# Three moves in the order of work of a state-space layer: softplus pieces, direct products, and spread ahead of decay

## The chip, the cores and the metric

The kernel runs on one core of a Trainium2 chip. The metric is the device time of one execution in microseconds (us), lower is better. The engines are TensorE (PE in the profile; PEld is its loading of weights), VectorE (DVE), ScalarE (ACT), GpSimd (POOL) and SyncE (SP), which issues the DMAs. Each works through its own queue in order and waits for others by semaphores.

## The reference

The input is x of shape (16, 128, 56, 56), all in float32. Two layers follow one another. The first is a block with a depthwise position convolution, layer norm, attention over windows of 8 by 8 pixels (each window attends to the four windows that fit it best), and an MLP. The change doesn't touch it. The second layer is:

```python
y = conv3x3(x) + conv_b                          # 128 -> 128 channels
seq = y.reshape(B * H * W, 8, 16)                # 50,176 sequences: 8 tokens of 16
out = mamba(seq)
out = group_norm(out, 4 groups) ; return x + silu(out)

def mamba(seq):
    xi, z = split(seq @ in_proj_w.T)             # 32 and 32
    xc = silu(causal_conv4(xi) + conv1d_b)
    dt, Bm, Cm = split(xc @ x_proj_w.T)          # 1, 16 and 16
    dt = softplus(dt * dt_proj_w + dt_proj_b)    # 32 per token
    dA  = exp(dt[..., None] * -exp(A_log))       # 32 x 16 per token
    dBx = dt[..., None] * Bm[:, :, None, :] * xc[..., None]
    h = 0
    for l in range(8):                           # the scan over the tokens
        h = dA[l] * h + dBx[l]                   # 32 x 16 states
        ys[l] = sum(h * Cm[l], over the 16)
    return ((ys + D * xc) * silu(z)) @ out_proj_w.T
```

## The kernel before

The first layer takes the first 3.2 ms of the span and the second layer the rest. The second layer (`layer1`, from line 711) works in 112 **row groups**: 16 images with 7 groups each (`g` 0 to 6), 448 sequences a group. A group's states at one token are 32 x 16 = 512 rows of 448, so four tiles of 128 partitions. They are worked on in two halves (`jp` 0 and 1) of two tiles each.

The main loop (lines 1192 to 1213) runs over groups `i` and, in each, over 14 **steps** `k`. Step `k` advances token `l = 1 + k // 2` in half `jp = k % 2`. Its work, in the order in which it is written and so queued:

- **advance** (lines 938 to 947, VectorE): the product `a * h` of the decay with the state of the token before (L946) and the add of the new input (L947). At token 7 (steps 12 and 13) a single product (L944) does it.
- **inject** for step `k + 4` (L936, VectorE): the spread product in PSUM times the gate Bm, written into a tile `h` as that token's new input.
- **decay** for step `k + 2` (L918, TensorE): dt times A into a PSUM tile `a`. There are two such tiles, so it waits until the advance of step `k` has read the older one.
- **spread** for step `k + 5` (L929, TensorE): dt * xc copied to the 128 rows of a tile. There is one PSUM tile `x`, so it waits for the inject of this step.
- **the exponential of the decay** (L921, ScalarE), in place in `a`.
- **weigh** at odd steps (L951, GpSimd): a token's state times the gate Cm, into `cst`.
- then what `work(i, k)` (lines 1077 to 1175) lists for the step, first VectorE's, then TensorE's, with the ScalarE work that reads their PSUM, then GpSimd's.

A decay and a spread of one step are four instructions each, two per tile of the half; each uses 32 rows of the array, and the two work on different halves.

`work` carries the current group `p`, the next one `nxt`, the one after that `far`, and older ones. For `nxt`:

- **rate** (lines 843 to 852, steps 1 and 2) is the dt product with wv into PSUM bank `pq0`, and ScalarE's absolute value `e` and positive part `dt`.
- **rate_exp** (854 to 857) and **rate_log** (859 to 862) are the rest of the softplus on ScalarE, two instructions each, for the two halves `h` of the tokens. **rate_sum** (864 to 870) is its four sums and products on GpSimd, at steps 6 and 8.
- **gate** (872 to 882, step 3) is the Bm and Cm products, ScalarE's two copies (L880) and their way through DRAM.
- **inner** (833 to 838) is a product into `pq0` and `pq1` and its SiLU on ScalarE: for `zs` of `nxt` at step 4 and for `xc` of `far` at step 12. A SiLU needs another activation table than exponentials and logarithms, so each call loads a table (L837), runs two SiLUs, and loads the first table back (L145).
- **product** (894, GpSimd, step 10) and **direct** (898 to 900, TensorE, step 13) prepare, for tokens 0 and 7, Bm * Cm summed over the 16 states, in bank `pq0`. **direct_mul** (902 to 908, two L905 on VectorE) multiplies it with dt * xc into `ud`.

For `p` and the group before it, **gather** (955 to 963, TensorE) sums `cst` over the states into `pq1`, **skip** (965) adds D * xc there, **collect** (970, VectorE) adds `ud`, **gated** (975, GpSimd) multiplies with silu(z) and **project_out** (980 to 1009) is the output product. One tap or two of the next image's 3x3 convolution (L787) stand on TensorE at steps 5 to 10. At an image's end group statistics and the normalisation come in: `group_mean` (L1027) and `group_var` (L1038) on TensorE, two large SiLUs (L1061) on ScalarE at step 12, and sums on GpSimd (L1068).

What sets the order is the order in which the program is written. `_chain` (lines 148 to 158) ties each engine's instructions to that order, SyncE's too; no planner moves them. The tiles `h` come from a pool of four. In the order of their first writing they are those of tokens 2, 3, 4, 5, 6, the next group's 0, then 7, then the next group's 1, and so on, so that the inject of step 12, which starts the next group's token 1, takes the tile of token 5.

Of the kernel before, what the change touches and what calls it, by code (L numbers as in the profile page):

```python
# [711 lines left out]
def layer1(ctx: ExitStack, tc: tile.TileContext, x1, t, out):  # L712
# [45 lines left out]
    for w, name in ((wx, "b_kx"), (wv, "b_dtw")):  # L758
        k = w1.tile(list(w.shape), F32, tag="fold", name=name)
# [124 lines left out]
    def bring(p, k, tokens):  # L884
        n = len(tokens)
        tile_ = w3.tile([P, 2, BLK], F32, tag="bc"[k] + "b", name=f"{'bc'[k]}b_{p['n']}_{tokens[0]}")
        src = p["dram", k][:, tokens[0] : tokens[0] + n, :].rearrange("s l n -> s (l n)")
        nc.sync.dma_start(
            tile_[:, 0:n, :].rearrange("p l n -> p (l n)"), src.unsqueeze(1).to_broadcast([16, 8, n * BLK])
        )  # L890
        for i, l in enumerate(tokens):
            p["gate", k, l] = tile_[:, i, :]
# [20 lines left out]
    def decay(p, l, jp):  # L913
        h, l4 = divmod(l, 4)
        a = p["a", l, jp] = ps_a.tile([P, 2, 512], F32, tag="a", name=f"a_{p['n']}_{l}_{jp}")[:, :, 0:BLK]
        for k in range(2):
            rows = slice(32 * (2 * jp + k), 32 * (2 * jp + k) + 32)
            nc.tensor.matmul(a[:, k, :], lhsT=adec[rows, l4, :], rhs=p["dt"][rows, h, :], start=True, stop=True)  # L918

    def decay_exp(p, l, jp):  # L920
        nc.scalar.activation(p["a", l, jp], p["a", l, jp], AF.Exp)  # L921
# [16 lines left out]
    def advance(p, l, jp):  # L938

        a, before = p["a", l, jp], p["h", l - 1][:, own(jp), :]  # L940
        if l == 7:
            if jp == 0:
                p["h", l] = w4.tile([P, 4, BLK], F32, tag="h", name=f"h_{p['n']}_{l}")
            nc.vector.tensor_mul(p["h", l][:, own(jp), :], a, before)  # L944
        else:
            nc.vector.tensor_mul(a, a, before)  # L946
            nc.vector.tensor_add(p["h", l][:, own(jp), :], a, p["h", l][:, own(jp), :])  # L947
# [129 lines left out]
    def work(i, k):  # L1077


        def at(n):  # L1080
            return groups[n] if 0 <= n < len(groups) else None

        p, nxt, far, prev = at(i), at(i + 1), at(i + 2), at(i - 1)
        pe, dve, pool = [], [], []
# [35 lines left out]
            pool.append(partial(store, three["b"], 1, k // 2 - 1))  # L1120

        if p:
            if k == 1:
                dve.append(partial(direct_mul, p))
            if k == 7:
                pe.append(partial(skip, p, 0))
            if k in (8, 9, 10):
                pe.append(partial(gather, p, k - 7))
            if k == 12:
                dve.append(partial(collect, p, 0))  # L1130
            if k == 13:
                pe += [partial(skip, p, 1), partial(gather, p, 4)]
                pool.append(partial(gated, p, 0))
            if k in (2, 6):
                bring(p, 0, {2: (4, 5), 6: (6,)}[k])
            if k in (1, 5, 9):
                bring(p, 1, {1: (3, 4), 5: (5, 6), 9: (7,)}[k])

        if nxt:
            if k in (1, 2):  # L1140
                pe.append(partial(rate, nxt, k - 1))
            if k in (2, 3):
                pe.append(partial(rate_exp, nxt, k - 2))
            if k in (3, 4):
                pe.append(partial(rate_log, nxt, k - 3))
            if k in (6, 8):
                pool.append(partial(rate_sum, nxt, k // 2 - 3))
            if k == 3:
                pe += [partial(gate, nxt, 0), partial(gate, nxt, 1)]
            if k == 4:  # L1150
                pe.insert(0, partial(inner, nxt, "zs", wz, w2, 0.0))
            if k == 7:
                bring(nxt, 0, (0, 1))
            if k == 8:
                bring(nxt, 1, (1, 2))
            if k == 11:
                bring(nxt, 0, (2, 3))
            if k == 10:
                pool.append(partial(product, nxt))
            if k == 13:  # L1160
                pe.append(partial(direct, nxt))

        if p and k in (5, 6, 7, 8, 9, 10) and p["b"] + 1 < NB:
# [28 lines left out]
    for i in range(-2, len(groups) + 3):  # L1192
        for k in range(14):
            now = 0 <= i < len(groups)
            if now:
                advance(*state_step(i, k))
            inputs = input_step(i, k + 4) if now or (i == -1 and k >= 10) else None
            if inputs:
                inject(*inputs)
            decays = state_step(i, k + 2) if now or (i == -1 and k >= 12) else None  # L1200
            if decays:
                decay(*decays)
            inputs = input_step(i, k + 5) if now or (i == -1 and k >= 9) else None
            if inputs:
                spread(*inputs)
            if decays:
                decay_exp(*decays)
            if now and k % 2:
                weigh(groups[i], 1 + k // 2)
            pe, dve, pool = work(i, k)  # L1210
            for part in (dve, pe, pool):
                for step in part:
                    step()
# [37 lines left out]
```

## Time and profile before

| | us |
|---|---|
| median of three runs | 8841.8 |
| lowest and highest | 8837.53 and 8855.01 |
| the profiled execution's own time | 8843.74 |
| its span, first to last instruction | 8841.9 |
| mean granted TensorE clock (1 is full) | 0.966 |
| first product of the first group's advance, from the span's start | 3250.8 |

The costliest groups of the second layer, as the profile lists them:

| line, engine | what | count | mean, ns |
|---|---|---|---|
| L951 POOL | weigh | 784 | 3996 |
| L936 DVE | inject | 1568 | 1083 |
| L946 DVE | advance, product | 1344 | 1091 |
| L947 DVE | advance, add | 1344 | 1092 |
| L921 ACT | exponential of the decay | 1568 | 900 |
| L918 PE | decay | 6272 | 606 |
| L929 PE | spread | 6272 | 608 |
| L787 PE | convolution tap | 2016 | 580 |

In a row of the timeline the first number is the start in us from the span's start and the second is the duration; in brackets stand the engine's idle time before the row and what ended it. A row with x2 or x4 has several like instructions merged, one behind the other. Where an engine is idle but another sets the pace, the idle time costs nothing.

### The profile page before, as it was taken

How to read it: one execution, taken by the hardware profiler on the slowest of the kernel's cores; microseconds unless marked ns; L12 is line 12 of the kernel's file. 1: busy time of each engine (PE TensorE's matmuls, PEld its weight loads, DVE VectorE, ACT ScalarE, POOL GpSimd, SP SyncE). 2: the span in 40 equal slices, each digit the busy share in tenths (PEclk: the TensorE clock that was granted, in tenths of full speed). 3: DMA queues.
4: the chain of work that ended last, by engine and by line, in shares of the span. 5: the costliest groups of instructions: out<-in, count | busy, mean ns of one | idle time of the engine just before them, and what ended most of it. 6: DMA issues, size and time to landing. Idle time of an engine off the chain costs nothing.

```text
span 8841.9 us, 151450 instructions
## 1 busy us (share of the span) xinstructions
PE 8013.1 (91%) x52860; PEld 3322.9 (38%) x52860; DVE 7764.8 (88%) x10358; ACT 5603.8 (63%) x10516; POOL 7035.4 (80%) x5664
## 2 busy tenths in 40 slices
PE   6999999999999879999999999999999999999987
PEld 3444444444444433333333333333333333333332
DVE  7999999999999839898898988988988989889887
ACT  4776777777777636666655665665656665666654
POOL 5878888878888328888888888888888888888887
PEclk8999999999999989999999999999999999999997
DMA  2333333333333222333333333333333333333332
GB/s 62 85 85 89 87 87 87 86 87 89 87 86 88 76 61 80 93 90 83 90 90 83 91 83 99 84 88 93 87 85 86 88 92 91 82 98 85 87 89 69
DMA packets 764424, 757.86 MB, mean 86 GB/s; under 512 B 188688, under 2 KB 663952, under 8 KB 761616
## 3 DMA queue, kind: packets, MB, share of 16 engines
q1 hardware_dynamic: 763664, 748.18, 32.8%
q8 instruction: 422, 6.91, 0.3%
q14 instruction: 338, 2.77, 0.1%
HBM read 439.61 MB, written 102.76 MB: 61 GB/s over the span
## 4 chain that ended last, share of the span: by engine, by line
PE 31%; ACT 24%; DVE 21%; POOL 11%; issue 10%; DMA 1%; SPq 0%; ACTq 0%; POOLq 0%; DVEq 0%
PE pq L787 8%; PE a L918 8%; ACT a L921 5%; DVE a L946 5%; DVE lepe L460 4%; DVE h L947 4%; POOL xh L263 4%; PE pq L960 4%; POOL e L379 4%; PE x L929 3%; ACT L837 3%; DVE h L936 3%; POOL tap L261 2%; ACT L145 2%; DVE sst L363 2%
## 5 line engine op out<-in xcount | busy, mean ns | idle before, releaser
L951 POOL TENSOR_TENSOR cst<-h,cb 128x1792 f32<-128x1792 f32 x784 | 3129.4, 3996 | 855.1 <-DVE h L947 580.4
L921 ACT ACTIVATE a<-a 128x896 f32<-128x896 f32 x1568 | 1404.3, 900 | 1772.7 <-PE x L929 1174.8
L936 DVE TENSOR_TENSOR h<-x,bb 128x896 f32<-128x896 f32 x1568 | 1697.6, 1083 | 276.9 <-PE x L929 145.6
L918 PE MATMUL a<-dt,adec 32*128 32x448 f32 x6272 | 1659.7, 606 | 214.4 <-DVE h L947 213.5
L946 DVE TENSOR_TENSOR a<-a,h 128x896 f32<-128x896 f32 x1344 | 1466.3, 1091 | 358.1 <-ACT a L921 357.5
L460 DVE SCALAR_TENSOR_TENSOR lepe<-vpad,lep,lepe 128x448 f32<-128x448 f32 x2688 | 1718.4, 678 | 0.6
L929 PE MATMUL x<-dtx,amask 32*128 32x448 f32 x6272 | 1664.8, 608 | 25.5 <-DVE h L936 24.5
L947 DVE TENSOR_TENSOR h<-a,h 128x896 f32<-128x896 f32 x1344 | 1467.0, 1092 | 45.8
L379 POOL TENSOR_SCALAR e<-e,sst,zero 128x256 f32<-128x256 f32 x1568 | 861.6, 560 | 451.4 <-DVE sst L375 396.6
L369 ACT ACTIVATE e<-ps,sst 128x256 f32<-128x256 f32 x1568 | 728.8, 469 | 544.5 <-DVE sst L363 493.6
L787 PE MATMUL pq<-x1pad,conv 128*128 128x448 f32 x2016 | 942.8, 580 | 59.5 <-ACT gst L1039 32.5
L918 PEld LDWEIGHTS a<-dt,adec 32*128 32x128 f32 x6272 | 484.2, 188 | 1247.4 <-DVE h L947 578.4
L263 POOL TENSOR_TENSOR xh<-xh,tap 128x448 f32<-128x448 f32 x735 | 841.4, 1145 | 42.5
L960 PE MATMUL pq<-cst,sel 128*32 128x448 f32 x6272 | 750.9, 564 | 1.5 <-POOL cst L951 1.5
L401 PE MATMUL ptt<-ident,e 128*128 128x128 f32 x3136 | 546.4, 285 | 92.3 <-POOL e L379 75.2
L363 DVE TENSOR_REDUCE sst<-ps 128x2 f32<-128x512 f32 x784 | 540.4, 689 | 86.3 <-PE ps L357 63.8
L929 PEld LDWEIGHTS x<-dtx,amask 32*128 32x128 f32 x6272 | 485.0, 189 | 339.8 <-DVE h L936 333.7
L357 PE MATMUL ps<-sel,q 32*64 32x256 f32 x6272 | 540.8, 413 | 68.2 <-ACT e L369 61.7
L261 POOL TENSOR_SCALAR tap<-xpad,pos,zero 128x448 f32<-128x448 f32 x735 | 533.6, 726 | 34.4
L787 PEld LDWEIGHTS pq<-x1pad,conv 128*128 128x128 f32 x2016 | 349.2, 194 | 497.4 <-issue 441.9
L401 PEld LDWEIGHTS ptt<-ident,e 128*128 128x128 f32 x3136 | 367.9, 142 | 416.5 <-POOL e L379 238.0
L407 ACT COPY att<-ptt 128x512 f32<-128x512 f32 x784 | 458.6, 585 | 48.0 <-PE ptt L401 40.3
(164 smaller groups left out, 12292.7 us busy)
## 6 DMA issues: line engine op xcount, KB each, us to landing
sel<-kv SPq DMA_DIRECT2D x3136, 64.0 KB
bb<-db SPq DMA_DIRECT2D x336, 448.0 KB
cb<-dc SPq DMA_DIRECT2D x336, 448.0 KB
xpad<-x SPq DMA_DIRECT2D x32, 784.0 KB
x<-r SPq DMA_DIRECT2D x112, 224.0 KB
x1pad<-x SPq DMA_DIRECT2D x16, 1568.0 KB
db<-bs SPq DMA_DIRECT2D x112, 224.0 KB
dc<-cs SPq DMA_DIRECT2D x112, 224.0 KB
```

The source lines that it names most:

```text
L263: nc.gpsimd.tensor_add(im["xh"][i], im["xh"][i], held["tap"])
L379: nc.gpsimd.tensor_scalar(e, e, im["st", w][:, 2, p : p + 1], zero, ALU.mult, ALU.add)
L460: nc.vector.scalar_tensor_tensor(out, src, lep[:, k : k + 1], acc, ALU.mult, ALU.add)
L787: nc.tensor.matmul(pc, lhsT=conv[:, k, :], rhs=pad[:, 8 * i + dy : 8 * i + dy + 8, dx : dx + W], start=(k == 0), stop=(k == 8),)
L918: nc.tensor.matmul(a[:, k, :], lhsT=adec[rows, l4, :], rhs=p["dt"][rows, h, :], start=True, stop=True)
L921: nc.scalar.activation(p["a", l, jp], p["a", l, jp], AF.Exp)
L929: nc.tensor.matmul(x[:, k, :], lhsT=mask[rows, l4, :], rhs=p["dtx"][rows, h, :], start=True, stop=True)
L936: nc.vector.tensor_mul(p["h", l][:, own(jp), :], px["x"], weight)
L946: nc.vector.tensor_mul(a, a, before)
L947: nc.vector.tensor_add(p["h", l][:, own(jp), :], a, p["h", l][:, own(jp), :])
L951: nc.gpsimd.tensor_mul(c, p["h", l], p["gate", 1, l].unsqueeze(1).to_broadcast([P, 4, BLK]))
L960: nc.tensor.matmul(py[32 * j : 32 * j + 32], lhsT=sel[:, l4, :], rhs=p["c", l][:, j, :], start=False, stop=(l % 4 == 3), skip_group_check= ...
```

## The change

There are three moves; no instruction is added or taken away.

- In the softplus of the next group, the first half's `rate_exp` stays at step 2 and its `rate_log` goes from step 3 to step 5. The second half's `rate_exp` goes from step 3 to step 6 and its `rate_log` from step 4 to step 7. `rate_sum` stays at steps 6 and 8.
- `direct_mul` goes from step 1 to step 0. `direct`, which makes its input, stays at step 13 of the group before, but ahead of that step's `skip` and `gather`. Only ahead of the very first group does it stand where it was.
- In each step of the main loop, `spread` is queued ahead of `decay`.

```diff
@@ work
         if p:
-            if k == 1:
+            if k == 0:
                 dve.append(partial(direct_mul, p))
...
             if k == 13:
+                if nxt:
+                    pe.append(partial(direct, nxt))
                 pe += [partial(skip, p, 1), partial(gather, p, 4)]
                 pool.append(partial(gated, p, 0))
...
         if nxt:
             if k in (1, 2):
                 pe.append(partial(rate, nxt, k - 1))
-            if k in (2, 3):
-                pe.append(partial(rate_exp, nxt, k - 2))
-            if k in (3, 4):
-                pe.append(partial(rate_log, nxt, k - 3))
+            if k in (2, 6):
+                pe.append(partial(rate_exp, nxt, k // 4))
+            if k in (5, 7):
+                pe.append(partial(rate_log, nxt, k // 2 - 2))
...
-            if k == 13:
+            if k == 13 and not p:
                 pe.append(partial(direct, nxt))
@@ the main loop
             decays = state_step(i, k + 2) if now or (i == -1 and k >= 12) else None
-            if decays:
-                decay(*decays)
             inputs = input_step(i, k + 5) if now or (i == -1 and k >= 9) else None
             if inputs:
                 spread(*inputs)
             if decays:
+                decay(*decays)
                 decay_exp(*decays)
```

## The prediction

> **What bounds it now.** I read the page first, then the busy times of one image's seven row groups, then the waits and the rows of one ordinary group. The page says that no engine is the limit throughout:
>
> ```profile
> PE 8013.1 (91%) x52860; PEld 3322.9 (38%) x52860; DVE 7764.8 (88%) x10358; ACT 5603.8 (63%) x10516; POOL 7035.4 (80%) x5664
> ...
> PE 31%; ACT 24%; DVE 21%; POOL 11%; issue 10%; DMA 1%; SPq 0%; ACTq 0%; POOLq 0%; DVEq 0%
> ```
>
> The chain hands over between four engines, so single waits count. The next view has busy time by stretch, one stretch per row group of the second layer (first product to first product):
>
> ```profile
> core 0: us, PE busy (x) PEld busy (x) DVE busy (x) ACT busy (x) POOL busy (x), PEclk, DMA share, GB/s
> ...
> 5728.02:5781.39 53.37, 47.99 (x237) 17.12 (x236) 44.23 (x46) 30.19 (x45) 41.63 (x25) 0.87 0.25 70
> 5781.39:5841.52 60.13, 50.97 (x233) 17.50 (x232) 45.18 (x48) 35.26 (x46) 47.49 (x23) 0.86 0.42 105
> ...
> 5888.93:5936.54 47.61, 45.24 (x236) 16.15 (x235) 44.71 (x48) 29.46 (x42) 40.32 (x19) 1.00 0.28 78
> ```
>
> Five of an image's seven groups are like the last (47.4 to 47.6 us, TensorE clock 1.00); two, after an image's end, are longer and run at 0.87 and 0.86. In the ordinary group VectorE works 44.7 of 47.6 us. Its waits there:
>
> ```profile
> DVE a L946 <- ACT a L921: 2.3, 2, 1.5
> DVE h L936 <- PE x L929: 0.2, 1, 0.2
> ```
>
> So two products wait for a decay exponential, 0.76 and 1.53 us. From here times of this group are us after its first product, at 5888.93. The rows of VectorE (timeline) give the places, steps 1 and 7, and where the direct products stand, behind step 1:
>
> ```profile
> 5892.90 1.10 DVE L946 TENSOR_TENSOR a<-a,h 128x896 f32<-128x896 f32 x1 [0.76 <-ACT a L921]
> ...
> 5896.04 1.27 DVE L905 SCALAR_TENSOR_TENSOR ud<-pq,vec,dtx 128x448 f32<-128x448 f32 x2
> ...
> 5915.02 1.10 DVE L946 TENSOR_TENSOR a<-a,h 128x896 f32<-128x896 f32 x1 [1.53 <-ACT a L921]
> ```
>
> ScalarE's rows say why step 7 is late: its exponential (first of the x2) stands behind a table load, two SiLUs, a load back, and two softplus pieces.
>
> ```profile
> 5908.53 0.92 ACT L921 ACTIVATE a<-a 128x896 f32<-128x896 f32 x1
> 5909.46 1.28 ACT L837 ACT_TABLE_LOAD   x1
> 5910.76 0.98 ACT L837 ACTIVATE zs<-pq 128x448 f32<-128x448 f32 x2
> 5911.76 1.28 ACT L145 ACT_TABLE_LOAD   x1
> 5913.05 0.67 ACT L861 ACTIVATE u<-u,neg 128x448 f32<-128x448 f32 x1
> 5913.63 0.56 ACT L862 ACTIVATE ln<-e 128x448 f32<-128x448 f32 x1
> 5914.09 1.70 ACT L921 ACTIVATE a<-a 128x896 f32<-128x896 f32 x2
> ```
>
> **The change, part by part.** It adds and removes no instruction; ACT, PE and DVE rows move. POOL's and SP's order stays, and each DMA keeps its place.
>
> *Spread ahead of decay.* Before, a decay product may start when its step's add is done, a spread product 1.0 us later, when the inject is done. Now the decay stands behind the spread and both start on the inject. They use different row strips and run side by side (rows at 5889.19 and 5889.20: both over in 1.03), so a spread ends as before and a decay ends about 1.0 later wherever TensorE used to wait; where TensorE was behind they already ran together and nothing changes. What waits behind is the step's exponential. In the ordinary group the exponentials of products 3, 4 and 5 end 2.3, 2.6 and 1.6 us before their products, so 1.0 is covered; product 6 had 0.8, but its exponential was held by ScalarE's queue, which is emptied below. Behind TensorE work at step 12 the decay moves from 5886.21 to 5886.5, so that the first SiLU burst and the exponential behind it (product 1) come 0.35 later: a cost of 0.35 if nothing fills it.
>
> *Direct products one step sooner.* Two L905 take 1.19 start to start (5896.04 to the product at 5897.23). They now stand between step 0's inject (ends 3.21) and product 1. That product waits until 3.97 now and until about 4.32 with the 0.35; the two L905 end the same gap at 4.32. Their TensorE product moves ahead of the skip, which waits for the second SiLU (5890.71); the direct one needs the first alone and is over near 2.6, before 3.1. So product 2, now at 8.30, comes at 4.33 + 3.13 (the distance of two products that do not wait, 5904.02 to 5907.15) = 7.46: a gain of 0.84. Without that cover the L905 cost their 1.19 at step 0 as they did at step 1: a loss of 0.35, the other end.
>
> *Softplus pieces.* Four rows of 0.5 to 0.65 leave step 3, two leave step 4; pairs go to steps 5, 6 and 7, where the exponentials now wait for TensorE 1.7 to 3.5 us. The chain to product 7: inject 8 ends 17.47 (0.84 earlier), spread and decay 1.09, exponential 0.95, so the first load starts at 19.53 (now 20.53); load 1.29, SiLUs 0.98, load 1.29, and directly the exponential, 23.11 to 24.01. Product 7 starts at 24.05 instead of 26.09: 2.04 in all, of which 1.20 is the softplus move. If the load stayed where it is, only the 1.04 of the two rows behind the SiLUs would come, and none if they merely came back ahead of a later exponential; step 8's is next and is needed 1 us after it ends.
>
> *What is late next.* GpSimd: its first softplus sum needs the logarithm's companion (L861), which now runs behind exponential 7 and ends at 24.7; GpSimd was free at 24.6 in the old frame and would be at 23.75. From the first sum's start to the end of cst of token 5 it is never idle (5913.54 to 5930.94: 17.4). The inject of step 12 reuses the h buffer which that cst reads. Now it ends at 42.0 and the inject starts at 44.07; with the change 24.75 + 17.4 = 42.15 against about 41.9, when VectorE and TensorE would be ready. So the inject comes at 42.2: 1.87 gained in this group, 1.65 in the 47.38 kind (inject at 43.85). TensorE's stretch from step 7 to 12 (3.55 a step, 5918.32 on) starts 2.05 earlier and is not the last. I take 1.75 a group. Ends: 2.04 (GpSimd in time) and 0.5 (head lost, burst mostly).
>
> *The two long groups of each image.* In the first TensorE idles 2.32 and runs at half speed behind it; I take 1.5, between 0 and 3.0 (this group takes 53.4 in some images, 50.3 in others). In the second, product 1 waits 6.65 behind the normalisation; the L905 move into that wait (1.19), but TensorE then works cold and the later decays no longer use its idle time: 0.7, between -1.0 and 2.4.
>
> *Sum.* 80 x 1.75 + 16 x (1.5 + 0.7) = 140 + 35 = 175. The profiled execution took 8843.7 (span 8841.9), 1.9 over the median of the three runs, 8841.8. 8841.8 - 175 = 8667.
>
> **The clock.** The row against this change is TensorE's clock:
>
> ```profile
> 5742.97 0.38 PE L1027 MATMUL pq<-mv,gmask 128*128 128x1 f32 x2 [1.31 <-ACT dt L852]
> ...
> 5744.54 3.08 PE L876 MATMUL pq<-xc,wbc 128*64 128x448 f32 x8
> ```
>
> After an idle time of 1.31 us the gate product takes 3.08 instead of 1.72 (5904.57). In the new order TensorE idles 1.0 to 1.1 at steps 2 and 3 of every group (dt product over at 12.8, next inject at 13.8), where it idled at most 0.5. For: the size. Against: it does the same products in a step of the same 3.13, only closer together, while around the 1.31 one spread came 3.6 after the other. The Trainium skill, TensorE: Matmul & The Clock Gate, section "Why this matters for your kernels", asks only that there be no idle gaps over about 3 us, as the clock falls after one idle window; by that rule an idle 1.1 costs nothing and the sum stays 8667, by the row above it may cost half a window or more. The trace does not agree with the page here, since 1.31 was enough.
>
> **Rivals.** (A) GpSimd takes the place more fully: its spans are rough, and each 0.1 us on that run of 17.4 costs 80 x 0.1 = 8 us. At 1 us more the gain is 0.75 a group: 8842 - 60 - 12 = 8770. For: it is packed from 24.6 to 51. Against: before step 6 it idles 1.6, 3.5 and 1.7 us a group. (B) Slower, by the clock: if it halves at steps 3 to 5 of every ordinary group, a stretch like the one above (slow from about 5743.9 to 5747.3, where the next pair is at full speed again: 3.4) costs TensorE 1.7, two cost 3.4. One just eats the 1.75; from two on it decides: 80 x 1.65 - 35 = +97, 8939. (C) Slower, by the later decays: direct products not ready (+0.35) and the burst no sooner because load and exponential wait for the decay: 112 x 0.35 = +39, 8881. It decides where a product's lead is under 1.0; only 6, of those not already waiting, is. (D) Nothing: the two waits are refilled by one another, 8842.
>
> **Numbers.** Chances: forecast 0.69, A 0.15, B 0.08, C 0.05, D 0.03. Faster 0.84, within 0.2% (18 us, about what a measurement tells from no change) 0.03, slower 0.13. The low end takes 2.04 a group and the upper bounds of the long ones: 163 + 86 = 249, 8593, rounded to 8590; the high end goes past A to 8790, leaving B, C and D out. The forecast's own range is 8600 to 8740.
>
> **What would show it.** Right: no wait at step 1 and about 0.4 at step 7; L905 straight behind step 0's inject; ordinary groups of 45.7 to 45.9; a short wait of step 12's inject for GpSimd; clock 1.00 there. Wrong: cold gate products (3.1) in ordinary groups, a wait at step 6, or exponential 7 waiting for L918.

## The result and the profile after

The changed kernel takes 8627.45 us (median of four runs, 8618.99 to 8630.68); the kernel before took 8841.59 beside it (8837.53 to 8855.01). The ratio is 0.9754, with a 95% interval from 0.9737 to 0.9771: faster by 214 us. The forecast was 8667, a gain of 175. The profiled execution has a span of 8617.2 us, 224.7 under the 8841.9 of before; all times taken from its rows are compared with that.

The page of the changed kernel, busy times and the shares of the chain that ended last:

```profile
PE 7449.8 (86%) x52860; PEld 3113.3 (36%) x52860; DVE 7758.7 (90%) x10358; ACT 5643.5 (65%) x10516; POOL 7025.9 (82%) x5664
...
DVE 32%; POOL 25%; PE 16%; ACT 13%; issue 12%; DMA 2%; SPq 0%; POOLq 0%; ACTq 0%; DVEq 0%
```

No engine has less work, but TensorE is busy for 563 us less (a spread and a decay that run side by side count once), and the chain has moved: TensorE's share fell from 31% to 16%, ScalarE's from 24% to 13%, and GpSimd's rose from 11% to 25%. The same by row group, for the three groups shown before the change (busy time of each engine, the granted TensorE clock, and the transfers):

```profile
core 0: us, PE busy (x) PEld busy (x) DVE busy (x) ACT busy (x) POOL busy (x), PEclk, DMA share, GB/s
5615.15:5664.04 48.89, 44.02 (x237) 15.48 (x236) 44.09 (x46) 30.32 (x45) 42.06 (x25) 0.93 0.28 76
5664.04:5720.19 56.15, 43.55 (x233) 15.07 (x232) 44.96 (x47) 35.34 (x46) 48.82 (x24) 0.91 0.45 112
...
5765.94:5811.69 45.75, 40.32 (x236) 14.22 (x235) 44.67 (x47) 29.80 (x42) 40.12 (x19) 1.00 0.30 81
```

The ordinary group (last row) went from 47.61 to 45.75, and VectorE works 44.7 of it. Its waits are down to two short ones:

```profile
DVE a L946 <- ACT a L921: 0.4, 1, 0.4
DVE h L936 <- POOL cst L951: 0.3, 1, 0.3
```

The wait at step 1 is gone and the one at step 7 fell from 1.53 to 0.38; a short one for GpSimd is new. VectorE's rows give the places (first number: start from the span's start; this group's first product starts at 5765.94):

```profile
5765.94 1.09 DVE L946 TENSOR_TENSOR a<-a,h 128x896 f32<-128x896 f32 x1
...
5769.07 1.26 DVE L905 SCALAR_TENSOR_TENSOR ud<-pq,vec,dtx 128x448 f32<-128x448 f32 x2
5770.31 1.10 DVE L946 TENSOR_TENSOR a<-a,h 128x896 f32<-128x896 f32 x1
...
5790.08 1.10 DVE L946 TENSOR_TENSOR a<-a,h 128x896 f32<-128x896 f32 x1 [0.38 <-ACT a L921]
...
5808.16 1.09 DVE L936 TENSOR_TENSOR h<-x,bb 128x896 f32<-128x896 f32 x1 [0.29 <-POOL cst L951]
```

The two direct products (L905) stand straight behind step 0's inject, product 1 follows them at 4.37 after the first, product 7 comes at 24.14, and the inject of step 12 at 42.22. ScalarE's rows of the burst in the same group:

```profile
5784.62 0.90 ACT L921 ACTIVATE a<-a 128x896 f32<-128x896 f32 x1 [1.52 <-PE a L918]
5785.56 1.28 ACT L837 ACT_TABLE_LOAD   x1
5786.86 0.98 ACT L837 ACTIVATE zs<-pq 128x448 f32<-128x448 f32 x2
5787.85 1.28 ACT L145 ACT_TABLE_LOAD   x1
5789.15 0.90 ACT L921 ACTIVATE a<-a 128x896 f32<-128x896 f32 x1
5789.96 0.66 ACT L861 ACTIVATE u<-u,neg 128x448 f32<-128x448 f32 x1
```

The exponential of step 7 now stands directly behind the load back, and the logarithm pieces behind it.

Where the 224.7 us lie, by the place of a row group in its image (mean from first product to first product; the long groups are the second and third places of an image, since the end of the image before is worked off there):

| groups | before, us | after, us | gain in all, us |
|---|---|---|---|
| 70 ordinary ones of the 14 inner images | 47.55 | 45.77 | 125 |
| second place of the 14 inner images | 51.58 | 48.19 | 48 |
| third place of the 14 inner images | 58.73 | 56.38 | 33 |
| first image, all seven | 48.31 | 45.78 | 18 |
| last image, first six | 48.98 | 48.88 | 1 |
| from the last group's first product to the end of the span | 86.51 | 85.23 | 1 |

The ordinary groups are what the forecast said. The long ones of these 14 images gained 80 us where it said 31 (35 for all 16), and that is the whole of the difference to the 224.7 us of the profile.

### The profile page after: what moved, and what is told of

It reads as the page before. It is cut to its first block, busy times and chain, and to the rows that moved or that the text cites. A ratio compares the mean times of both kernels' runs of the same rounds, so it can differ in the third digit from the quotient of the medians.

```text
span 8617.2 us, 151466 instructions
## 1 busy us (share of the span) xinstructions
PE 7449.8 (86%) x52860; PEld 3113.3 (36%) x52860; DVE 7758.7 (90%) x10358; ACT 5643.5 (65%) x10516; POOL 7025.9 (82%) x5664
## 4 chain that ended last, share of the span: by engine, by line
DVE 32%; POOL 25%; PE 16%; ACT 13%; issue 12%; DMA 2%; SPq 0%; POOLq 0%; ACTq 0%; DVEq 0%
DVE h L936 10%; DVE a L946 7%; POOL cst L951 5%; PE x L929 5%; POOL xh L263 5%; POOL e L379 4%; DVE h L947 4%; DVE lepe L460 3%; POOL tap L261 3%; ACT a L921 3%; POOL dtx L870 2%; PE pq L960 2%; PE pq L787 2%; ACT L145 2%; DVE sst L363 2%
## 5 line engine op out<-in xcount | busy, mean ns | idle before, releaser
L947 DVE TENSOR_TENSOR h<-a,h 128x896 f32<-128x896 f32 x1344 | 1467.2, 1092 | 46.1
```

## The experiments

The theory to test is the prediction's own: the gain is the sum of a shorter burst (softplus), a filled wait (direct products), and next to nothing for the spread, until GpSimd is late. The rivals are that one move carries all of it, and that TensorE's clock decides (rival B). Each run below says how it differs from the changed kernel or from the one before. Each time stands beside one of the kernel before, measured on the same chip: 8841.0 for the three runs with one move undone and the early logarithm, 8853.8 for the run with TensorE kept busier and the three with one move alone, 8842.0 for the next three, 8851.5 for the last. Between these sets the ratios are compared.

### One move undone

**Without the softplus move.** The changed kernel, with:

```diff
-            if k in (2, 6):
-                pe.append(partial(rate_exp, nxt, k // 4))
-            if k in (5, 7):
-                pe.append(partial(rate_log, nxt, k // 2 - 2))
+            if k in (2, 3):
+                pe.append(partial(rate_exp, nxt, k - 2))
+            if k in (3, 4):
+                pe.append(partial(rate_log, nxt, k - 3))
```

> The changed kernel with the softplus pieces back where they were (rate_exp at steps 2 and 3, rate_log at 3 and 4); direct products and spread as changed. My theory: the direct products alone are worth 0.84 us per ordinary group net of the later decay, the softplus move the rest. Then step 1 has no wait, step 7 waits about 1.5 again, ordinary groups take 46.7 to 46.8, and the whole 8740 (8715 to 8775). Rival 1, the softplus move is all of it: 8820 or more, ordinary groups 47.5. Rival 2, spread ahead of decay carries the gain of the two long groups of each image (48.4 and 56.4 against 51.6 and 58.8): these keep their new times here, and the whole is 8690 or less.

Measured: 8840.6, ratio 1.0003 (0.999 to 1.0016). A plain miss: without the softplus move, the other two gain nothing at all. The mean ordinary group takes 47.66 (47.55 before), the second place of an image 52.25 (51.58) and the third 57.44 (58.73). Two neighbouring ordinary groups show why (columns as above):

```profile
5833.40:5880.09 46.69, 40.16 (x233) 14.12 (x232) 43.78 (x46) 29.31 (x42) 39.73 (x19) 1.00 0.27 78
5880.09:5928.42 48.33, 41.96 (x236) 14.77 (x235) 44.77 (x48) 29.43 (x42) 40.55 (x19) 0.96 0.30 78
```

The first is near what the theory of waits gives; the second lost a stretch of TensorE's clock. TensorE's rows of the two groups at step 7, the warm one first:

```profile
5862.09 0.65 PE L929 MATMUL x<-dtx,amask 32*128 32x448 f32 x2 [1.65 <-DVE h L936]
...
5863.05 1.02 PE L966 MATMUL pq<-xc,dd 128*128 128x448 f32 x2
...
5908.78 1.12 PE L929 MATMUL x<-dtx,amask 32*128 32x448 f32 x2 [1.66 <-DVE h L936]
...
5910.59 1.81 PE L966 MATMUL pq<-xc,dd 128*128 128x448 f32 x2
```

In both, product 7 is late (it waits 1.65 for its exponential), so the inject behind it is late, and with it TensorE, in one piece of 1.65 or 1.66 us. The same idle time left the clock at full speed in one group and halved it in the other. Of the 60 ordinary groups of the twelve middle images 27 ran without such a stretch, in 46.7 to 46.9 us, 32 had one of 3.4 us and one had two; those with one took 48.2 to 48.4, some 1.4 to 1.7 more. In the whole second layer TensorE spent 592 us at half speed here, 444 before and 345 in the changed kernel.

The trace tells the two kinds of group apart. All 248 changes of the clock in this run lie, within 0.02 us, on one grid with a step of 3.413 us over the whole span. Of the 60 pieces of idle time at step 7, the 32 that began 1.13 to 2.05 us behind a mark of this grid were all followed by a half-speed stretch; of the 28 that began elsewhere, one was.

**The same with TensorE kept busier.** That the clock is the cause of the lost time is still an argument at this point. So the run above, with two products at step 6 that nothing reads:

```diff
+    def fill(n):
+        for _ in range(n):
+            nc.tensor.matmul(
+                pq[1][:, 256:512], lhsT=ident, rhs=wx.rearrange("p h n -> p (h n)"), start=True, stop=True
+            )
...
+            if k == 6:
+                pe.append(partial(fill, 2))
```

> The run with the old softplus place, direct products and spread as changed, and in step 6 of every group, ahead of the output product, two products more on TensorE that nobody reads (identity against 256 columns of the wx weights, into columns of pq1 that the output product then overwrites). It computes everything the others do, and those two besides. Theory, the clock is the reason why that run gained nothing: some 1.1 us more work takes the idle 1.66 at step 7 down to about 0.5, the clock stays full, ordinary groups take 46.7 to 46.8 and the whole is faster by the extra work, 8770 (8740 to 8800). Rival, the clock follows from something else: ordinary groups 47.5 to 48.1 as there, or slower by the extra products, 8840 to 8930.

Measured: 8750.2, ratio 0.9881 (0.986 to 0.9903). With more work than the run before it, it is 1.2% faster. The rows of an ordinary group and of its step 7 (the line numbers are higher by 6: L935 is the spread, L942 the inject):

```profile
5841.70:5888.62 46.92, 41.26 (x240) 14.98 (x239) 44.67 (x47) 29.47 (x42) 40.28 (x19) 1.00 0.29 79
...
5870.38 0.64 PE L935 MATMUL x<-dtx,amask 32*128 32x448 f32 x2 [0.79 <-DVE h L942]
```

The idle time is cut to 0.79, none of the 60 groups has a half-speed stretch, and they take 46.7 to 46.9 throughout. So rival B's mechanism is real, at step 7 rather than at the steps 3 to 5 where the prediction looked for it. The added products both shorten the idle piece and add work to the window; the run doesn't tell these two apart. In the changed kernel the softplus move keeps the stretches out, by cutting product 7's wait to 0.38; TensorE then idles 0.62 there (before the spread at 5793.36).

**Without the direct products' move.** The changed kernel, with `direct_mul` back at step 1 and `direct` back behind step 13's `skip` and `gather`:

```diff
-            if k == 0:
+            if k == 1:
                 dve.append(partial(direct_mul, p))
...
             if k == 13:
-                if nxt:
-                    pe.append(partial(direct, nxt))
                 pe += [partial(skip, p, 1), partial(gather, p, 4)]
...
-            if k == 13 and not p:
+            if k == 13:
                 pe.append(partial(direct, nxt))
```

> The changed kernel with the direct product and its two VectorE instructions back where they were (direct behind skip and gather at step 13, direct_mul at step 1); softplus and spread as changed. My theory: the wait at step 1 is back and longer by the 0.35 that the later decay costs, 1.1 us; product 7 then comes 0.85 sooner than before the change instead of 2.04, the run of GpSimd up to the inject of step 12 leaves some 0.55 of it, ordinary groups take 46.9 to 47.1, the whole 8755 (8730 to 8790). Rival, the direct products only moved a wait: 8640 or less. In the long group behind the normalisation the 1.19 come back: 57.6 or more there.

Measured: 8747.5, ratio 0.9897 (0.9871 to 0.9924), as expected. The third place takes 57.37, just under the 57.6 that was the least expected. Ordinary groups take 46.95, which is 1.18 over the changed kernel: the two L905, 1.19 start to start. An ordinary group's waits:

```profile
DVE a L946 <- ACT a L921: 1.5, 2, 1.1
DVE h L936 <- POOL cst L951: 1.1, 1, 1.1
```

Product 1 waits 1.15 on average where it waited 0.76 in the ordinary group shown before the change (0.71 on average), since its decay comes later behind the spread: 0.39 against the 0.35 of the prediction. That is the gap which the L905 fill.

TensorE's rows of the same groups matter for the clock:

```profile
5891.03 0.64 PE L929 MATMUL x<-dtx,amask 32*128 32x448 f32 x2 [1.44 <-DVE h L936]
```

An idle piece of 1.44 stands in each of the 60 ordinary groups here, and in none of them did the clock fall.

**Without the spread's move.** The changed kernel, with the decay queued first again:

```diff
             decays = state_step(i, k + 2) if now or (i == -1 and k >= 12) else None
+            if decays:
+                decay(*decays)
             inputs = input_step(i, k + 5) if now or (i == -1 and k >= 9) else None
             if inputs:
                 spread(*inputs)
             if decays:
-                decay(*decays)
                 decay_exp(*decays)
```

> The changed kernel with decay queued ahead of spread again; softplus and direct products as changed. My theory: in the ordinary group nothing that sets the pace hangs on it, since the two L905 fill the gap in front of product 1 either way and the second table load waits for the product with wz, behind both: 45.7 to 45.8 as in the changed kernel. Neutral in all: 8627, within 15. Rival 1, it carries the gain of the long groups (fewer stretches at half clock): ordinary groups 45.8, long ones 50 to 51 and 58, the whole 8670 to 8700. Rival 2, the later decays cost: faster than 8605.

Measured: 8604.4, ratio 0.9729 (0.9701 to 0.9757). This interval overlaps that of the changed kernel (0.9737 to 0.9771). Ordinary groups take 45.70 in place of 45.77, as the theory said; the total is below its 8612 to 8642 and just within what the second rival asked for (under 8605). So with the other two moves in place, the spread's move buys nothing in the ordinary groups. In the total it may cost up to some 20 us, which is too little to be told. TensorE is busy for 7959 us here, 509 more than in the changed kernel: most of that fall in busy time comes from this move, and it bought no time.

### GpSimd as what is late next

In the changed kernel the run of GpSimd's work from the first softplus sum to the `cst` of token 5 is unbroken, from 24.76 to 42.19 after the first product. GpSimd's rows, its first and last ones:

```profile
5790.70 1.13 POOL L867 TENSOR_TENSOR u<-u,e 128x448 f32<-128x448 f32 x1 [0.91 <-ACT u L861]
...
5804.13 4.00 POOL L951 TENSOR_TENSOR cst<-h,cb 128x1792 f32<-128x1792 f32 x1
```

The changed kernel, with the first half's logarithm back at step 3, so that this sum doesn't wait for it:

```diff
-            if k in (5, 7):
-                pe.append(partial(rate_log, nxt, k // 2 - 2))
+            if k in (3, 7):
+                pe.append(partial(rate_log, nxt, k // 4))
```

> The changed kernel with one pair of the softplus pieces, the first half's rate_log, back at step 3; the rest stays deferred. My theory: in the changed kernel the inject of step 12 waits for GpSimd (0.3 to 1.0 us), whose run of 17.4 us starts when that rate_log is done behind the exponential of step 7. ScalarE has room for it at step 3 (1.15 us between the exponential of product 5 and the product with wz), so GpSimd starts 1.0 us sooner and the first table load does not move: ordinary groups 45.3 to 45.5, the whole 8597 (8585 to 8615). Rival 1, GpSimd is not the limit and the inject waits for something else: 45.8 and 8627. Rival 2, the pair pushes the copies of the gate and with them the product with wz and the first table load: product 7 up to 1.1 later, 46.5 or more, 8690.

Measured: 8593.1, ratio 0.9724 (0.9691 to 0.9756). Ordinary groups take 45.42 to 45.66, 0.24 less on average, and the inject of step 12 waits for another engine:

```profile
5847.48 1.09 DVE L936 TENSOR_TENSOR h<-x,bb 128x896 f32<-128x896 f32 x1 [0.72 <-PE a L918]
```

It waited 1.05 for GpSimd in the groups of this kind and now waits 0.72 for TensorE. So GpSimd was the limit by 0.1 to 0.35 us a group, with TensorE close behind. The ratio's interval overlaps that of the changed kernel; the ordinary groups are what tells the two apart.

### One move alone

Each of these is the kernel before with one of the three moves.

The direct products alone:

```diff
-            if k == 1:
+            if k == 0:
                 dve.append(partial(direct_mul, p))
...
             if k == 13:
+                if nxt:
+                    pe.append(partial(direct, nxt))
                 pe += [partial(skip, p, 1), partial(gather, p, 4)]
...
-            if k == 13:
+            if k == 13 and not p:
                 pe.append(partial(direct, nxt))
```

> The kernel before with the direct products one step sooner, and nothing else (decay ahead of spread, softplus where it was). The run with both order changes and the old softplus place gained nothing, though its row groups behind the two long ones took 46.7: its other ordinary groups took 47.5 to 48.1 and held a stretch of half clock each, behind 1.66 us in which TensorE was idle at step 7 without a break. Theory now: with decay ahead of spread the decay starts 1.0 sooner and breaks that idle time, so the clock stays at 1.00, the ordinary groups take 46.7 to 46.8, and the whole 8755 (8730 to 8780). Rival, the clock falls here too, as the same products stand in the same time: 8840.

Measured: 8766.5, ratio 0.9903 (0.988 to 0.9925); ordinary groups 46.86 against 47.55, a gain of 0.68. In four of the 60 ordinary groups of the middle images the clock fell, as it did in four of the kernel before, each time behind an idle piece of no more than 0.77. The wait at step 7 stays:

```profile
DVE a L946 <- ACT a L921: 1.6, 1, 1.6
```

The softplus alone:

```diff
-            if k in (2, 3):
-                pe.append(partial(rate_exp, nxt, k - 2))
-            if k in (3, 4):
-                pe.append(partial(rate_log, nxt, k - 3))
+            if k in (2, 6):
+                pe.append(partial(rate_exp, nxt, k // 4))
+            if k in (5, 7):
+                pe.append(partial(rate_log, nxt, k // 2 - 2))
```

> The kernel before with the softplus pieces moved, and nothing else. Theory: product 7 comes 1.2 sooner, the wait of product 1 stays at 0.72, the clock stays full in the ordinary groups, GpSimd's run leaves about 0.9 of the 1.2: 46.5 to 46.7 in an ordinary group, the whole 8720 (8695 to 8750). Rival, it needs the other two: 8790 or more.

Measured: 8680.7, ratio 0.9808 (0.9786 to 0.9829), better than expected. Ordinary groups took 46.37, a gain of 1.18. The unexpected part is in the second place of an image: 48.22 against 51.58, with 38 us at half speed over all images in place of 109. What ended there shows in the section on the long groups.

The spread alone:

```diff
-            if decays:
-                decay(*decays)
             inputs = input_step(i, k + 5) if now or (i == -1 and k >= 9) else None
             if inputs:
                 spread(*inputs)
             if decays:
+                decay(*decays)
                 decay_exp(*decays)
```

> The kernel before with spread queued ahead of decay, and nothing else. Theory: the later decay puts the first SiLU burst of each group back by 0.35 and with nothing to fill it product 1 with it; and at step 7 TensorE idles 1.66 in one piece, so that many ordinary groups hold a stretch of half clock (1.4 us each): 48 to 49.3 in an ordinary group, the whole 8900 (8860 to 8960). Rival 1, no cost: 8842, within 15. Rival 2, the order alone helps (spread sooner at the injects that wait for it): 8820 or less.

Measured: 8910.2, ratio 1.0062 (1.004 to 1.0085): slower. Two ordinary groups:

```profile
5914.13:5965.08 50.95, 43.63 (x236) 15.13 (x235) 44.80 (x48) 29.45 (x42) 40.15 (x19) 0.93 0.27 70
5965.08:6014.45 49.37, 41.89 (x233) 14.60 (x232) 43.99 (x45) 29.33 (x42) 40.11 (x19) 0.97 0.27 76
```

Two things add up. Product 1 waits 1.15 on average where it waited 0.71, which by an estimate is 35 us over 80 groups; and the clock falls more often, in ordinary groups like these too (533 us at half speed in all, 444 before).

Alone, the three moves give -173, -87 and +56 us, -204 together; all at once they gave -214. Undone singly, beside 8841.0 for the kernel before in place of 8841.6, they are worth 213 (softplus), 120 (direct) and about nothing (spread, -23).

### What the long groups hide

The second place of an image has only a few distinct lengths, and the clock goes with them. Two such groups of the kernel before, and then two of the changed one:

```profile
3986.44:4036.90 50.46, 44.41 (x237) 16.04 (x236) 43.96 (x45) 30.08 (x45) 41.58 (x25) 0.97 0.27 74
4683.93:4737.26 53.33, 47.80 (x237) 17.13 (x236) 44.32 (x46) 30.14 (x45) 41.27 (x25) 0.87 0.24 66
```

```profile
3949.02:3995.86 46.84, 40.81 (x237) 14.80 (x236) 43.99 (x45) 30.33 (x45) 41.19 (x25) 1.00 0.29 79
4280.70:4332.62 51.92, 47.05 (x237) 16.80 (x236) 44.23 (x45) 30.32 (x45) 43.47 (x26) 0.87 0.27 71
```

Before, each of the 14 inner images had at least one stretch of 3.4 us at half speed there: eight had one (0.97) and six three or four (0.90 to 0.87). After, eight had none and took 46.8, three had one or two, three had four.

One idle piece of TensorE in this group changed with the softplus move. Step 7's convolution tap waits for ScalarE's part of the group variance (L1039). The first row is from the group of 53.37 us in the prediction, the second from the first of the two groups after:

```profile
5755.36 1.86 PE L787 MATMUL pq<-x1pad,conv 128*128 128x448 f32 x2 [2.32 <-ACT gst L1039]
```

```profile
3973.36 1.02 PE L787 MATMUL pq<-x1pad,conv 128*128 128x448 f32 x2 [1.28 <-ACT gst L1039]
```

L1039 stood behind the same two softplus pieces as the exponential of step 7. In all five kernels that have these pieces in the old place the idle time is 2.32 in all 14 second places, and all of them have a half-speed stretch. In the kernels with the moved pieces it is 1.28, and some have none. How many is not decided by this piece alone: 8 of 14 in the changed kernel, 11 with the early logarithm, 2 in the run `merged` below.

The next two runs were made from the run with the early logarithm. First, the decay ahead of the spread again, since undoing either had not cost anything:

```diff
+            if decays:
+                decay(*decays)
             inputs = input_step(i, k + 5) if now or (i == -1 and k >= 9) else None
             if inputs:
                 spread(*inputs)
             if decays:
-                decay(*decays)
                 decay_exp(*decays)
```

> The changed softplus and direct moves, with the first half's logarithm back at step 3 and the decay ahead of the spread as before the change. If GpSimd's late first sum and the late decay are two separate costs, the gains of the two runs that took away one each add up: 8593 less some 20 = 8573 (8560 to 8590), ordinary groups at 45.3 to 45.5, the group behind an image's end under 47.1. If both runs gained by the same thing, TensorE's warmer clock in the group behind an image's end, they don't add up: 8593 again, within 8.

Measured: 8644.0, ratio 0.978 (0.9761 to 0.9798). A miss for both expectations: slower than the run it came from. Ordinary groups took 45.47 (45.53 there); the second place went from 47.09 to 48.79 with 92 us at half speed in place of 38, and the third from 57.90 to 59.07 with 218 in place of 174. The decay ahead, which had lost nothing in the changed kernel, loses 0.6% here, in the long groups alone. Against the changed kernel the two edits together lose 0.3%, with intervals that overlap.

The second took on the wait that the changed kernel has left at an image's end, 5.9 at product 1 of the third place, behind the SiLUs of the normalisation. Those of the next input stand right in front, and each of the two has a pair of table loads. The two now share one pair:

```diff
-    def inner(p, which, w, pool, bias):
+    def inner(p, which, w, pool, bias, back=True):
...
-        _act_set(tc, EXP_LN)
+        if back:
+            _act_set(tc, EXP_LN)
...
-                pe.insert(0, partial(inner, far, "xc", wx, w3, c1_b))
+                pe.insert(
+                    0,
+                    partial(inner, far, "xc", wx, w3, c1_b, back=not (two and two["g"] == NBLK - 1)),
+                )
```

> As the run before it, and behind an image's end the SiLUs of the next input and those of the normalisation share one pair of table loads: one load back and one load (1.28 each) are left out per image, on the way to the exponential of product 1, which waits 5.9 there. Theory (that wait is ScalarE's queue and on the path): 16 x 2.56 = 41 less than the run before it, about 8532 (8520 to 8555), and the wait of product 1 at 3.3. Rival (what comes next in that group, the wait of step 8's inject for the transfer of the b gate, takes it back): under 15 less, with that wait at 5 to 6 in place of 3 to 4.

Measured: 8591.4, ratio 0.9708 (0.9687 to 0.9729), 53 less than the run before it, whose edit it keeps; 41 were expected. The 8532 expected for the whole were missed, since that run had come out 71 above its own forecast. The waits in a third place (line numbers are one higher here, L947 is the product, L937 the inject):

```profile
DVE h L937 <- PE x L930: 4.1, 3, 1.7
DVE h L937 <- DMA bb<-db: 3.9, 1, 3.9
DVE a L947 <- ACT a L922: 3.1, 2, 2.7
```

The product's wait fell to 2.7, and the next is the transfer of a Bm gate at 3.9 (2.8 in the changed kernel). SyncE stands long at one load of this place, here in the changed kernel:

```profile
SPq L1052 <- POOL xr L1068: 22.8, 1, 22.8
```

That load is the residual's; it waits for GpSimd, and the theory of the next run took it for the cause. The rows of SyncE's queue in `merged` (L1053 is that load, L883 the gates' way to DRAM, L1072 to L1074 the stores of the finished image, L889 the fetches of the gates) and VectorE's late inject speak for another:

```profile
5668.24 0.47 SPq L1053 DMA_DIRECT2D res<-x  x1
...
5684.88 0.63 SPq L883 DMA_DIRECT2D dc<-cs  x1
5685.60 0.53 SPq L1072 DMA_DIRECT2D out<-xr  x1
5686.18 0.79 SPq L1073 DMA_DIRECT2D out<-xr  x1
5687.02 2.44 SPq L1074 DMA_DIRECT2D out<-xr  x1
5689.50 2.23 SPq L889 DMA_DIRECT2D cb<-dc  x1
5691.83 3.20 SPq L889 DMA_DIRECT2D bb<-db  x2
```

```profile
5699.15 1.09 DVE L937 TENSOR_TENSOR h<-x,bb 128x896 f32<-128x896 f32 x1 [3.90 <-DMA bb<-db]
```

The residual's load is issued 16 us before the gates are ready. What stands between the gates' way out and their fetch is the three stores, which hold the queue from 5685.60 to 5689.46. The next run fetches the residual at step 3 of the next group, when GpSimd has long been done, and adds it later; the stores follow the last addition, so they move too:

```diff
-                pool += [partial(store, b, 0, 0), partial(store, b, 0, 1), partial(residual, b, 1)]
+                pool += [partial(store, b, 0, 0), partial(store, b, 0, 1)]
...
-        if three and three["g"] == NBLK - 1 and k in (2, 4):
-            pool.append(partial(store, three["b"], 1, k // 2 - 1))
+        if three and three["g"] == NBLK - 1:
+            if k == 3:
+                residual(three["b"], 1)
+            if k in (10, 12):
+                pool.append(partial(store, three["b"], 1, k // 2 - 5))
```

> As the run before it, and the second half's residual is fetched at step 3 of the next group in place of step 13, and added at steps 10 and 12 of that group. Theory (step 8's inject waits 3 to 4 for a gate's transfer because SyncE's queue stands at the residual until GpSimd has stored the first half): that wait goes, at most 12 to 16 x 3.5 = 42 to 56 less, about 8490 (8470 to 8525). Rival (GpSimd is late at step 12 there by the two additions of 1.85): half of it is lost to a wait of step 12's inject of 1.5 to 3, 8510 to 8535.

Measured: 8554.7, ratio 0.9675 (0.9658 to 0.9692), 37 less, where 42 to 56 less were expected. The same place again:

```profile
DVE a L947 <- ACT a L922: 3.1, 2, 2.7
DVE h L937 <- PE x L930: 2.1, 2, 1.9
```

The transfer's wait is gone and the third place takes 50.26 in place of 56.06. From the gates' way out to the end of the issue of `bb` it is now 3.2 us (5657.24 to 5660.42), where it was 9.5 in `merged` (5685.51 to 5695.03). The load, the additions and the stores moved together; that the stores are what counts is read from the rows and not shown by a run of its own. The group behind it gave 1.5 back (46.93 in place of 45.39), and the second place lost 0.6, with more time at half speed (150 us in place of 119).

Last, the spread ahead of the decay in that kernel, the one edit:

```diff
-            if decays:
-                decay(*decays)
             inputs = input_step(i, k + 5) if now or (i == -1 and k >= 9) else None
             if inputs:
                 spread(*inputs)
             if decays:
+                decay(*decays)
                 decay_exp(*decays)
```

> As the run merged_residual, and the spread stands ahead of the decay as in the change, which is the one edit. With the first half's logarithm at step 3 the order decided the clock of the group behind an image's end: 38 us at half speed and 47.1 a group with the spread ahead, 92 us and 48.8 with the decay ahead. Theory (the order decides that group's clock here too, where it now has 150 us and 50.25 a group): 47 to 48 a group, 16 x 2.2 to 3.2 less, about 8510 (8495 to 8530), half speed in that group under 60 us. Rival (the clock there falls by small shifts of any edit, and the order means nothing by itself): within 20 of 8555, or slower.

Measured: 8520.2, ratio 0.9632 (0.9608 to 0.9656): the fastest of all, 3.7% under the kernel before. The second place took 48.51 (50.25 without the edit) with 82 us at half speed (150), the third 49.48 (50.26) with 61 (102). The total is what the theory expected (8495 to 8530); the second place and its clock lie between the two expectations. The order of spread and decay does work on the clock of the long groups, but less than it did with the early logarithm alone.

## Why the prediction was right, and where it was not

**Ordinary groups: right, by the mechanism and the size.** The head was to gain 0.84 and the burst 1.20; alone they gave 0.68 and 1.18. Product 2 was to come at 7.46 and came at 7.51 (8.30 before). Product 7 was to come at 24.05 and came at 24.14; the inject of step 12 at 42.2 and came at 42.22; GpSimd's run of 17.4 took 17.43. The two kinds of group were to gain 1.87 and 1.65; those of 47.61 gained 1.84 and those of 47.38 gained 1.62. The mean is 1.78 against 1.75. That GpSimd would be late next, and by how little, is shown by the run with the early logarithm, where the wait at step 12 passes to TensorE. Rival A, 1 us more of it, did not come.

**Later decays: right.** The 0.35 at product 1 measured 0.39 where nothing fills it (the run without the direct products' move). Products 3 to 6 do not wait.

**The clock: right for this kernel, for a reason that was narrower than the text had it.** TensorE idles 1.05 and 0.97 in one piece behind steps 2 and 3 as foreseen, and in none of the 60 ordinary groups of the middle images did the clock fall:

```profile
5779.84 0.65 PE L929 MATMUL x<-dtx,amask 32*128 32x448 f32 x2 [1.05 <-DVE h L936]
...
5783.50 0.65 PE L929 MATMUL x<-dtx,amask 32*128 32x448 f32 x2 [0.97 <-DVE h L936]
```

But rival B was not far off: with the other two moves and without the softplus one, it ate their whole gain. The prediction read its row of 1.31 us as enough for a stretch. That is too simple: the same 1.31 stands in all 14 second places of the changed kernel, and in eight of them the clock stays full. A piece of 1.44 was harmless in 60 groups, while one of 0.77 was followed by a stretch in four groups of the kernel before. Where a piece lies on the grid of 3.413 us counts as well. The Trainium skill's rule (TensorE: Matmul & The Clock Gate, section "Why this matters for your kernels": no idle gap over about 3 us) would have let 1.66 pass; the measurement decides: 33 of those 60 groups had a half-speed stretch. What the Trainium skill says on the same page in its section "What's actually happening", that the activity is judged in windows of 3413 ns which run freely, whatever the kernel does, agrees with the trace: the clock changes on a grid of this step alone, and the same idle 1.65 is harmless in one group and not in the next.

**The two long groups: the term that was mis-sized.** The prediction took 1.5 and 0.7 us, 31 for the 14 inner images; they gave 3.4, above its upper bound of 3.0, and 2.35, 80 in all. For the second place it saw the idle 2.32 and the half speed behind it, but gave the ordinary group's 1.75 a small cut and left the clock as it was. It did not see that the pieces which leave the burst also stand ahead of L1039, so that the 2.32 becomes 1.28. By the runs the clock did not stay: half-speed time there went from 109 to 61 us over all images, 3.4 for each inner image, one stretch. At the 1.4 to 1.7 which a stretch cost in the ordinary groups, an estimate of the gain is 1.78 + 1.5 = 3.3, and 3.4 was measured. The softplus move does it, as its run alone shows (51.58 to 48.22). In the third place the wait of product 1 fell from 6.65 to 5.9 and half-speed time from 205 to 165; no single move alone gives the whole 2.35 there, and that part stays open.

**The spread: costed at next to nothing, and in this company that held.** Alone it costs 56 us: the later decays of rival C, at 0.39 to 0.44 in an ordinary group, and more half-speed time (533 us against 444). Why the order helps in the long groups with the early logarithm and shows no gain with the late one stays open.

The first image gained 17.7 us and the last, to the end of the span, 1.9, where the sum has 10.95 for each (5 x 1.75 + 1.5 + 0.7); that the two nearly cancel is luck.

## What to carry to other kernels

Count the waits of the engine that works nearly all the time in a typical group, follow each to the queue that is late, and then look for what comes next: here that gave the gain of 70 groups to 0.03 us each, on average. Then look at the groups that are not typical, and at the TensorE clock in each of them separately: an edit that ends one wait can end a half-speed stretch with it, or cause one, and that is worth as much as the wait. An order that costs nothing beside one set of moves can cost time beside another, so the combination has to be run.

## What the runs showed of the hardware

- Idle TensorE time of 1.65 to 1.77 us in one piece was followed by a half-speed stretch of 3.4 us in 33 of 60 like groups. Pieces of 1.03 to 1.06 us were in none of 60, in three kernels, and pieces of 1.44 us in none of 60, in another; but one of 0.77 us was in four groups of the kernel before. So the length of a piece alone does not decide. Two more products ahead of the 1.66, which cut it to 0.79, took all of these stretches in those groups away, and with more work the kernel was 1.2% faster.
- In each of the 14 kernels all changes of the TensorE clock lie on one grid of 3.413 us, within 0.02 us from the start of the span to its end. A piece of 1.65 to 1.77 us that began 1.13 to 2.05 us behind a mark of the grid was followed by a stretch in 32 of 32 cases, one that began elsewhere in 1 of 28.
- A half-speed stretch cost such a group 1.4 to 1.7 us, though VectorE sets its pace: TensorE has little to spare there (40 of 46 us busy).
- SyncE's share of the chain that ended last is given as 0%, yet what stands ahead in its queue can set a wait: behind three stores that held it for 3.9 us a gate's fetch came 3.9 us late for VectorE. In the run where the stores came later, together with the residual's load and the additions in front of them, that wait was gone and the kernel 37 us faster.
